# Two Flamingo layers on one core: in layer 1, sums of exponentials added on DVE, block inputs kept in DRAM, a third free PSUM bank

## The chip, the cores and the metric

The kernel runs on one core of a Trainium2 chip. The metric is the device time of one execution in microseconds (us); shorter is better. The time before is the median of three runs, 2996.78 us (2994.19 to 2997.82).

## The reference

The input x holds 8 sequences of 512 tokens with 256 channels in fp32, and a context of 512 tokens with 128 channels for each. Two layers follow each other; each adds a gated attention part and a gated feed-forward part. All of the change lies in layer 1, whose two parts compute, cut to what matters:

```python
def _mha(x, y, ..., causal):
    xn = _ln(x, lnx_g, lnx_b)
    yn = _ln(y, lny_g, lny_b)
    q, k, v = (16 heads of 32 from xn, yn, yn)
    a = softmax(q @ k.T * 32 ** -0.5, axis=-1)
    if causal:
        a = a * mask              # keys t > s are kept; after the softmax, so its sum runs over all keys
    o = a @ v                     # heads side by side: 512 channels
    x_out = x + o @ li1_w + li1_b
    h = gelu(_ln(x_out, ln3_g, ln3_b) @ li2_w + li2_b)      # 256 -> 1024
    return x_out + h @ li3_w + li3_b                        # 1024 -> 256

x = _ln(xx, ln1_g, ln1_b)
x = x + _mha(x, x, a1..., causal=True)       # block 0
x = _ln(x, ln2_g, ln2_b)
x = x + _mha(x, ctx, a2..., causal=False)    # block 1

# feed-forward part of layer 1: quantised 256 -> 1024, a convolution over
# three tokens in each channel, silu, quantised 1024 -> 256
```

## The kernel before

Everything is in fp32 but the quantised products, which are exact in bf16. A sequence's 512 tokens are 4 tiles of 128. Layer 0 is computed first (to about 925 us); what layer 1 needs of it lies in DRAM: `hd` (layer 0's hidden activations), `kd` and `vd` (keys and values of the context for block 1), and the three copies of x in `xd`.

Layer 1 works through 16 slots, one per sequence and block, in the order that `slot_of` gives: sequences 0 and 1 in block 0, the same two in block 1, then 2 and 3, and so on. One slot's attention (`steps1`) has 16 steps: 4 groups `g` of 4 heads, and in each of them 4 key tiles `n`. A step has a front and a back. The front is four products of 32 rows, one per head, into two PSUM tiles `ps_s` of two banks each, then two exponentials on ACT (L2070) into `pt`, a tile of 128 keys x 4 heads x 512 queries (8 KB in each partition, three buffers), and in block 0 a select on POOL (L2074) that masks the diagonal piece into `dg`. The back is, per head, a product of `pt` with 32 columns of ones into `sm` (the softmax's sum, repeated over 32 rows) and the products with the values into `ov`. After the fourth key tile the sum is turned on DVE (L2106), inverted (L2107), turned back (L2109) and multiplied onto `ov` (L2111), which gives `oT`.

Beside the attention run streams of other work, each a generator that yields before it needs something:

- `first(b)`: the end of layer 0's feed-forward part for sequence b; it stores x (`store_x`, L1792).
- `pre1(b, half)`: layer 1's entry for half a sequence: load x, layer normalisation, the block's input `res`, then `enter1`: scale and shift of the normalisation, the inner normalisation, the bias of `li1` added into `res` (L1911), and the turned input `zT`; then the values `vt`.
- `pair1(b, blk, g)`: queries and keys `QT`, `KT` of a head group.
- `mlp1(b, blk, half)`: `oT` times `li1` plus `res` into `xo` (L1978), normalisation, `li2`, gelu, `li3`, added to `res`; at the end of block 0 it goes on through `enter1` to block 1.
- `last(b)`: the feed-forward part of layer 1. A loop over eight channel tiles f: product, scaling into a padded tile `hp` (L2164), and three steps of the convolution (L2167 or L2172, then twice L2176).

`weave_all` puts all of it into one order for each engine while the program is built. It asks a planner (`Pace`) that holds an estimate of when each engine is free, when each tile is done and when the next buffer of a ring is free. Of the candidates that could start within 0.3 us on PE it takes the one with the lowest place: `base + share * done / total` for a stream, the slot and step number for the attention. Where an evacuation may go to ACT or DVE, `sooner` picks by the planner's free times. At most two fronts may be ahead of the backs.

[...] four in `st1` (`ps_s`), two in `ac1` (`sm`, `ov1`), two in `m1a`, the ring `m1` from which `bank()` serves every other product. All DMAs of layer 1 are issued from SP's queue, in program order.

Of the kernel before, what the change touches and what calls it, by code (L numbers as in the profile page):

```python
# [8 lines left out]
F32 = mybir.dt.float32  # L9
# [922 lines left out]
class Fast(General):  # L932
# [8 lines left out]
    def setup(self, ctx, ctx0):  # L941
        super().setup(ctx, ctx0)
        nc, tc = self.nc, self.tc
        dram = ctx.enter_context(tc.tile_pool(name="dram", bufs=1, space=bass.MemoryType.DRAM))

        def scratch(name, shape, dtype=F32):
            return [dram.tile(shape, dtype, name=f"{name}{b}") for b in range(B)]


        self.xd = [scratch(f"xd{k}_", [P, NT * C]) for k in range(3)]  # L950
        self.hd = scratch("hd", [P, NF * T])
        self.cd = scratch("cd", [P, T])
        self.kd = scratch("kd", [P, 4 * T])
        self.vd = scratch("vd", [P, NT * 2 * C])
        self.fwd = {
            n: dram.tile([P, 2 * FF], BF16, name=f"q_{n}")
            for n in ("f0_w1", "f0_w2", "f1_w1", "f1_w2")
        }
        keep = self.keep2
        self.ones = keep.tile([P, 32], F32, name="ones")  # L960
        nc.vector.memset(self.ones, 1.0)


        self.ext = keep.tile([P, 2, 3 * B], F32, name="ext")
        self.n_ext = 0
        self.seqs, self.units, self.given = {}, {}, set()
        self.rest = self.coming = None
        self.behind = Behind()
        self.pace = Pace(tc)
        self.pace.open()  # L970
# [687 lines left out]
    def layer1_xattn(self):  # L1658
        nc, tc = self.nc, self.tc
        with (  # L1660
# [6 lines left out]
            tc.tile_pool(name="m1a", bufs=2, space=PSUM) as self.m1,  # L1667
# [4 lines left out]
            self.hps = [[wpool.tile([P, T // 2 + 2], F32, name=f"hp{k}_{i}") for i in range(2)] for k in range(2)]  # L1672
            for t in self.hps[0] + self.hps[1]:
                nc.gpsimd.memset(t, 0.0)
# [4 lines left out]
            self.li1s, self.mlps, self.loads = [0, 0], [0, 0], {}  # L1679
# [10 lines left out]
            for k, (b, blk) in enumerate(order):  # L1690
                for half in range(2):
                    mlps[half].append(Stream(self.mlp1(b, blk, half), 20.5, 0.88 if blk else 0.65, k + 1))
                    if not blk:
                        pres[half].append(Stream(self.pre1(b, half), 7.5, 0.88, k - 1))
                for g in range(4):
                    pairs.append(Stream(self.pair1(b, blk, g), 3.0, 0.2, k + 0.25 * (g - 1)))
# [100 lines left out]
    def first(self, b):  # L1797
# [32 lines left out]
        yield need(x, pe=False)  # L1830
        self.store_x(1, b, x)
        self.given.add((1, b))
# [40 lines left out]
    def pre1(self, b, half):  # L1873

        while (1, b) not in self.given:
            yield WAIT
# [3 lines left out]
        while b > 2 and self.mlps[half] <= self.slot_of(b - 3, 1):  # L1880
            yield WAIT
        res = q["res", half] = work.tile([P, 2, C], F32, tag=f"res{half}", name="res", bufs=3)
        yield from self.ln_timed(x, res, f"p{half}", of_ln=True)
        yield from self.enter1(b, half, "ln1", "a1", x, f"p{half}")
# [16 lines left out]
    def enter1(self, b, half, ln, pre, z, of):  # L1901
# [3 lines left out]
        res = q["res", half]  # L1905
# [5 lines left out]
        nc.gpsimd.tensor_tensor(res, res, self.row1b(f"{pre}_li1_b"), ALU.add)  # L1911
        blk = int(pre == "a2")
# [13 lines left out]
        if self.both(b, ("zT in", blk)):  # L1926
            q["zT", blk] = zT

# [32 lines left out]
    def mlp1(self, b, blk, half):  # L1961
# [3 lines left out]
        pre = ("a1", "a2")[blk]  # L1965
        while ("oT", blk, 3) not in q:
            yield WAIT
        res = q["res", half]
# [72 lines left out]
        yield from self.enter1(b, half, "ln2", "a2", z, f"m{half}")  # L2041
        self.mlps[half] += 1

    def steps1(self, b, blk):
# [37 lines left out]
        def back(g, n):  # L2082
            self.backs += 1
            kt, pt, parts = st.pop((g, n))
            if n == 0:
                st["sm"] = self.ovp.tile([P, T], F32, tag="sm", name="sm")
                st["ov"] = self.ovp.tile([P, T], F32, tag="ov1", name="ov")
            ov, sm = st["ov"], st["sm"]
            for j in (2, 3, 0, 1):
                self.mm(sm[32 * j : 32 * j + 32, :], self.ones, pt[:, j, :], n == 0, n == NT - 1)  # L2090
            for i, (p, cols) in enumerate(parts):
                for j in (2, 3, 0, 1):
# [5 lines left out]
                    )  # L2098
            if n < NT - 1:
                return  # L2100

# [8 lines left out]
            oT = q["oT", blk, g] = work.tile([P, T], F32, tag="oT", name="oT", bufs=6)  # L2110
# [4 lines left out]
        def back_at(g, n):  # L2115

            if n == NT - 1 and min(self.li1s) < (4 * slot + g - 2) // 4:
                return 1e9
            _, pt, parts = st[g, n]
            t = pace.when([Pace.name(pt), Pace.name(q["vt", blk])] + [Pace.name(p) for p, _ in parts])  # L2120
            return t if n else max(t, pace.place("sm"), pace.place("ov1") - 1.1)
# [7 lines left out]
    def last(self, b):  # L2129
# [25 lines left out]
        for half in range(2):  # L2155

            to = slice(1 - half, n + 2 - half)
            cols = slice(half * (n - 1), half * (n - 1) + n + 1)
            h = work.tile([P, NF, n], F32, tag="hF", name="hF")
            for f in range(NF):  # L2160
                hp = self.hps[half][f % 2]
                yield need(ur, xq, *([h] if f else []))
                ps = self.proj(w1, xq, f * P, cols)
                nc.vector.tensor_tensor(hp[:, to], ps, ur[:, cols], ALU.mult)  # L2164
                a = h[:, f, :]
                if self.pace.sooner(0.47, 0.46):
                    nc.scalar.activation(  # L2167
                        a, hp[:, 0:n], AF.Identity,
                        scale=self.col("conv_w", 3 * f), bias=self.col("conv_b", f),
                    )  # L2170
                else:
                    nc.vector.tensor_scalar(  # L2172
                        a, hp[:, 0:n], self.col("conv_w", 3 * f), self.col("conv_b", f), ALU.mult, ALU.add
                    )
                for k in (1, 2):
                    nc.vector.scalar_tensor_tensor(  # L2176
                        a, hp[:, k : k + n], self.col("conv_w", 3 * f + k), a, ALU.mult, ALU.add
                    )
# [163 lines left out]
```

## Time and profile before

| | us |
|---|---|
| median of three runs | 2996.78 |
| the profiled execution, its own time | 3002.77 |
| its span, from the first to the last instruction | 3001.0 |
| PE busy | 2614.2 (87%) |
| ACT busy | 1488.5 (50%) |
| DVE busy | 1426.5 (48%) |
| POOL busy | 524.2 (17%) |
| PE busy on products with ones (2048 records) | 273.8 |

The profile is of one execution and 6.0 us longer than the median. An fp32 product shows as two records, so the 2048 records are 1024 products, in 256 groups of four [...]. Their busy time counts the stretch in which at least one of them runs; the end of a record is modelled and can lie under the next product. The busy shares are means over stages: up to 800 us layer 0's attention, then layer 0's feed-forward part, from 1000 to 2808 us layer 1 with its attention, then a tail without any.

The page's second part shows the span in 40 slices of 75 us (tenths):

```profile
PE   5999999999682998999988999998989998899842
DVE  2334444434474335334355664345663425665455
ACT  2666665656572445444444545444544344545321
PEclk9999999999896999999999999999999999999965
```

### The profile page before, as it was taken

To read this page: it belongs to the slowest core of one execution; us is meant where nothing else is said; L and a number is where in the kernel's file an instruction comes from. 1 tells how busy PE (TensorE), PEld (TensorE's weight loads), DVE (VectorE), ACT (ScalarE), POOL (GpSimd) and SP (SyncE) were. 2 spreads that over 40 slices of the span, in tenths; PEclk is the share of its full clock that TensorE was granted. 3 is DMA by queue.
4 is the path that set the end of the run, shared out by engine and by line. 5 is a ranking of instruction groups with operands and counts; after the bars stand their busy time and mean duration, and the time that the engine had idled before them with its cause. 6 is when DMAs were issued, how large, how long until landed. Compare 5 with 4: busy or idle time off the path is not lost.

```text
span 3001.0 us, 39948 instructions
## 1 busy us (share of the span) xinstructions
PE 2614.2 (87%) x16359; PEld 1226.4 (41%) x16364; DVE 1426.5 (48%) x2899; ACT 1488.5 (50%) x1817; POOL 524.2 (17%) x687
## 2 busy tenths in 40 slices
PE   5999999999682998999988999998989998899842
PEld 2333333333231344444544435454444454444531
DVE  2334444434474335334355664345663425665455
ACT  2666665656572445444444545444544344545321
POOL 2111111111001224112221111231110201201100
PEclk9999999999896999999999999999999999999965
DMA  3011110100275203201200212110110110110110
GB/s 104 8 40 46 46 40 29 39 15 12 91 308 203 71 15 102 74 22 64 77 27 8 74 56 93 64 43 8 64 39 25 43 57 8 57 46 18 43 35 15
DMA packets 67663, 167.20 MB, mean 56 GB/s; under 512 B 6416, under 2 KB 35472, under 8 KB 59664
## 3 DMA queue, kind: packets, MB, share of 16 engines
q1 hardware_dynamic: 65248, 161.89, 15.4%
q8 instruction: 130, 2.13, 0.3%
q0 software_dynamic: 640, 2.10, 0.2%
q10 hardware_dynamic: 1584, 0.58, 0.1%
q14 instruction: 61, 0.50, 0.1%
HBM read 110.02 MB, written 54.53 MB: 55 GB/s over the span
## 4 chain that ended last, share of the span: by engine, by line
PE 72%; DVE 15%; ACT 7%; issue 3%; DMA 2%; POOL 1%; SPq 0%; ACTq 0%; DVEq 0%; POOLq 0%
PE ps L1010 35%; PE ps_s L1010 17%; PE ov L1010 11%; PE sm L1010 7%; DVE hext L1618 2%; PE ps L1013 2%; DVE hF L2176 2%; ACT pt L1369 1%; ACT pt L2070 1%; DVE mv L1841 1%; DVE hm L2184 1%; ACT hF L2167 1%; DVE oT L2111 1%; DVE hp L2164 1%; DVE rb L2109 1%
## 5 line engine op out<-in xcount | busy, mean ns | idle before, releaser
L1010 PE MATMUL ps_s<-QT,KT 32*128 32x512 f32 (+3 forms) x4096 | 607.0, 611 | 79.6 <-ACT QT L1953 25.7
L2070 ACT ACTIVATE pt<-ps_s 128x1024 f32<-128x1024 f32 x512 | 495.7, 1020 | 303.2 <-PE ps_s L1010 300.3
L1369 ACT ACTIVATE pt<-ps_s 128x1024 f32<-128x1024 f32 (+3 forms) x512 | 411.8, 861 | 206.1 <-PE ps_s L1010 200.3
L1010 PEld LDWEIGHTS ps_s<-QT,KT 32*128 32x128 f32 x4096 | 191.3, 186 | 380.1 <-issue 197.4
L1010 PE MATMUL sm<-pt,ones 128*32 128x512 f32 x2048 | 273.8, 606 | 0.2 <-DVE rt L2106 0.2
L1010 PE MATMUL ps<-x3T,li 128*128 128x256 f32 x1024 | 253.5, 392 | 20.8 <-DVE hD L1652 13.8
L1010 PE MATMUL ov<-pt,v 128*32 128x512 f32 (+3 forms) x2048 | 238.9, 537 | 13.2 <-POOL pt L1372 12.9
L1010 PE MATMUL ps<-li,hD 128*128 128x256 f32 x1024 | 239.1, 387 | 5.6 <-ACT hD L2020 4.3
L1010 PEld LDWEIGHTS ps<-x3T,li 128*128 128x128 f32 x1024 | 186.2, 191 | 106.1 <-issue 37.3
L1010 PEld LDWEIGHTS ps<-li,hD 128*128 128x128 f32 x1024 | 190.9, 191 | 68.0 <-issue 26.2
L1010 PE MATMUL ov<-pt,vt 128*32 128x512 f32 (+3 forms) x1792 | 192.8, 501 | 2.6 <-DVE oT L2111 2.6
L2074 POOL TENSOR_SCALAR_AFFINE_SELECT dg<-pt 128x512 f32<-128x512 f32 x128 | 85.8, 671 | 582.9 <-ACT pt L2070 582.9
L1652 DVE TENSOR_SCALAR hD<-ps,cols 128x256 f32<-128x256 f32 x178 | 81.2, 481 | 203.8 <-PE ps L1010 113.5
L1372 POOL TENSOR_SCALAR_AFFINE_SELECT pt<-pt 128x512 f32<-128x512 f32 x128 | 87.1, 680 | 482.6 <-ACT pt L1369 482.6
L2176 DVE SCALAR_TENSOR_TENSOR hF<-hp,cols,hF 128x256 f32<-128x256 f32 x256 | 131.6, 514 | 61.1 <-ACT hF L2167 54.9
L1847 POOL TENSOR_SCALAR mv<-mv 128x2 f32<-128x2 f32 (+1 forms) x104 | 25.6, 246 | 767.7 <-DVE mv L1842 724.3
L2167 ACT ACTIVATE hF<-hp,cols 128x256 f32<-128x256 f32 x82 | 49.2, 600 | 202.0 <-DVE hp L2164 202.0
L1010 PE MATMUL ps<-zT,a_wq 128*128 128x512 f32 x256 | 130.6, 635 | 9.7 <-DVE hD L1652 5.1
L1010 PE MATMUL ps<-li,oT 128*128 128x256 f32 x512 | 128.7, 395 | 7.5 <-DVE oT L2111 5.9
L1010 PE MATMUL ps<-fw,hq 128*128 128x256 bf16 x512 | 71.5, 300 | 67.1 <-DVE hq L1822 54.6
L1650 ACT ACTIVATE hD<-ps,cols 128x256 f32<-128x256 f32 x78 | 36.6, 473 | 176.1 <-PE ps L1010 152.3
L1394 DVE STREAM_TRANSPOSE ot<-ov 128x512 f32<-128x512 f32 x64 | 45.8, 716 | 158.5 <-PE ov L1010 158.5
(252 smaller groups left out, 3404.7 us busy)
## 6 DMA issues: line engine op xcount, KB each, us to landing
hd<-h SPq DMA_DIRECT2D x16, 1024.0 KB, 3.9
hF<-hd SPq DMA_DIRECT2D x16, 1024.0 KB, 6.5
li<-in_w_a_dram SPq DMA_DIRECT2D x16, 1024.0 KB, 5.0
fw<-q_f_w SPq DMA_DIRECT2D x24, 512.0 KB, 5.8
xF<-xd SPq DMA_DIRECT2D x24, 512.0 KB, 5.1
kd<-k SPq DMA_DIRECT2D x8, 1024.0 KB, 3.9
vd<-v SPq DMA_DIRECT2D x8, 1024.0 KB, 4.4
vt<-vd SPq DMA_DIRECT2D x8, 1024.0 KB, 6.2
```

The lines of the kernel that those rows point to most:

```text
L1010: self.nc.tensor.matmul(out, lhsT, rhs, start=start, stop=stop, skip_group_check=True)
L1013: self.nc.tensor.transpose(out, in_, self.ident)
L1369: nc.scalar.activation(pt[:, 2 * jp : 2 * jp + 2, lo:], pss[jp][:, :, lo:], AF.Exp)
L1372: nc.gpsimd.affine_select(out=diag, in_=diag, compare_op=ALU.is_ge, fill=0.0, base=0, pattern=[[0, 4], [1, P]], channel_multiplier=-1,)
L1394: nc.vector.transpose(ot.rearrange("p b d -> p (b d)"), ov)
L1618: nc.vector.tensor_reduce(e, hh, AX.X, op)
L1650: self.nc.scalar.activation(out, ps, AF.Identity, bias=bias)
L1652: self.nc.vector.tensor_scalar(out, ps, bias, None, ALU.add)
L2070: nc.scalar.activation(pt[:, 2 * jp : 2 * jp + 2, :], pss[jp], AF.Exp)
L2074: nc.gpsimd.affine_select(out=dg, in_=pt[:, :, diag], compare_op=ALU.is_gt, fill=0.0, base=0, pattern=[[0, 4], [-1, P]], channel_multiplier=1,
L2167: nc.scalar.activation(a, hp[:, 0:n], AF.Identity, scale=self.col("conv_w", 3 * f), bias=self.col("conv_b", f),)
L2176: nc.vector.scalar_tensor_tensor(a, hp[:, k : k + n], self.col("conv_w", 3 * f + k), a, ALU.mult, ALU.add)
```

## The change

The sum over key tiles is split: DVE adds the first three `pt` of a head group into a tile of its own, `acc`, and PE multiplies only `acc` and the fourth `pt` with ones, both after the last product with the values. `sm` is no longer a bank of its own; it comes from the ring `m1`, which has three banks now. A `pt` that waits for its add stays in its buffer.

Room in SBUF for `acc` (8 KB in each partition) comes from `res`, which had three buffers for each half: `pre1` and `mlp1` now write the block's input to DRAM (`rd`), and the next `mlp1` loads it into a single buffer; from `oT` (five buffers, not six, with the condition in `back_at` moved by one head group); and from `hp` (two tiles, not four; both halves use the same ones, with the reads shifted by `half` in place of the write). `first` stores each half of x as soon as it is done, and `pre1` waits for its own half. Two shares of the streams change: `mlp1` in block 0 from 0.65 to 0.5, `pre1` from 0.88 to 0.65.

```diff
--- before.py
+++ after.py
@@ -948,6 +948,8 @@
         self.xd = [scratch(f"xd{k}_", [P, NT * C]) for k in range(3)]
+
+        self.rd = scratch("rd", [P, NT * C])
         self.hd = scratch("hd", [P, NF * T])
         self.cd = scratch("cd", [P, T])
         self.kd = scratch("kd", [P, 4 * T])
@@ -1664,19 +1666,19 @@
             tc.tile_pool(name="small2", bufs=1) as self.small,
             tc.tile_pool(name="st1", bufs=2, space=PSUM) as self.st,
             tc.tile_pool(name="ac1", bufs=1, space=PSUM) as self.ovp,
-            tc.tile_pool(name="m1a", bufs=2, space=PSUM) as self.m1,
+            tc.tile_pool(name="m1a", bufs=3, space=PSUM) as self.m1,
         ):
             self.work = work
             self.seqs = {b: {} for b in range(B)}
-            self.hps = [[wpool.tile([P, T // 2 + 2], F32, name=f"hp{k}_{i}") for i in range(2)] for k in range(2)]
-            for t in self.hps[0] + self.hps[1]:
+            self.hps = [wpool.tile([P, T // 2 + 3], F32, name=f"hp{i}") for i in range(2)]
+            for t in self.hps:
                 nc.gpsimd.memset(t, 0.0)
             self.wl = {}
             self.pairs = self.fronts = self.backs = self.zTs = self.nvt = 0
-            self.li1s, self.mlps, self.loads = [0, 0], [0, 0], {}
+            self.li1s, self.mlps, self.loads, self.both_in = [0, 0], [0, 0], {}, {}
             order = [(2 * p + k, blk) for p in range(B // 2) for blk in range(2) for k in range(2)]
             few, pairs, mlps, pres = [], [], [[], []], [[], []]
@@ -1689,9 +1691,9 @@
             few.sort(key=lambda s: s.base)
             for k, (b, blk) in enumerate(order):
                 for half in range(2):
-                    mlps[half].append(Stream(self.mlp1(b, blk, half), 20.5, 0.88 if blk else 0.65, k + 1))
+                    mlps[half].append(Stream(self.mlp1(b, blk, half), 20.5, 0.88 if blk else 0.5, k + 1))
                     if not blk:
-                        pres[half].append(Stream(self.pre1(b, half), 7.5, 0.88, k - 1))
+                        pres[half].append(Stream(self.pre1(b, half), 7.5, 0.65, k - 1))
                 for g in range(4):
                     pairs.append(Stream(self.pair1(b, blk, g), 3.0, 0.2, k + 0.25 * (g - 1)))
             self.weave_all([self.steps1(b, blk) for b, blk in order], [few, pairs, *mlps, *pres])
@@ -1827,9 +1829,8 @@
                     self.mm(ps[:, k, :], hq[:, f, k * P : (k + 1) * P], w2[:, f, :], f == 0, f == NF - 1)
             x2 = x[:, 2 * half : 2 * half + 2, :]
             nc.vector.scalar_tensor_tensor(x2, ps, self.sg, x2, ALU.mult, ALU.add)
-        yield need(x, pe=False)
-        self.store_x(1, b, x)
-        self.given.add((1, b))
+            self.store_x(1, b, x2, half)
+            self.given.add((1, b, half))
     def ln_timed(self, x, out, of, of_ln=False):
@@ -1872,16 +1873,14 @@
     def pre1(self, b, half):
-        while (1, b) not in self.given:
+        while (1, b, half) not in self.given:
             yield WAIT
         nc, work, q = self.nc, self.work, self.seqs[b]
         x = self.load_x(1, b, f"xP{half}", half)
         yield need(x, pe=False)
-        while b > 2 and self.mlps[half] <= self.slot_of(b - 3, 1):
-            yield WAIT
-        res = q["res", half] = work.tile([P, 2, C], F32, tag=f"res{half}", name="res", bufs=3)
+        res = work.tile([P, 2, C], F32, tag=f"resP{half}", name="resP")
         yield from self.ln_timed(x, res, f"p{half}", of_ln=True)
-        yield from self.enter1(b, half, "ln1", "a1", x, f"p{half}")
+        yield from self.enter1(b, half, "ln1", "a1", res, x, f"p{half}")
         while "vt" not in q and (self.nvt < self.slot_of(b, 0) or self.backs < 16 * (self.slot_of(b, 0) - 1)):
             yield WAIT
         if "vt" not in q:
@@ -1898,17 +1897,17 @@
         if self.both(b, "pre1"):
             q["vt", 0] = vt
-    def enter1(self, b, half, ln, pre, z, of):
+    def enter1(self, b, half, ln, pre, res, z, of):
         nc, work, q = self.nc, self.work, self.seqs[b]
-        res = q["res", half]
         nc.vector.tensor_tensor(res, res, self.row1b(f"{ln}_g"), ALU.mult)
         yield need(res, pe=False)
         nc.gpsimd.tensor_tensor(res, res, self.row1b(f"{ln}_b"), ALU.add)
         yield need(res, pe=False)
         yield from self.ln_timed(res, z, of)
         nc.gpsimd.tensor_tensor(res, res, self.row1b(f"{pre}_li1_b"), ALU.add)
+        nc.sync.dma_start(self.half_of(self.rd[b], half), res.rearrange("p t c -> p (t c)"))
         blk = int(pre == "a2")
         while ("zT of", blk) not in q and (self.zTs < self.slot_of(b, blk) or self.pairs < 4 * (self.slot_of(b, blk) - 1)):
             yield WAIT
@@ -1925,6 +1924,7 @@
             nc.vector.tensor_copy(at, ps)
         if self.both(b, ("zT in", blk)):
             q["zT", blk] = zT
+            self.both_in[b, blk] = 2
     def slot_of(self, b, blk):
@@ -1963,9 +1963,12 @@
         nc, work, q = self.nc, self.work, self.seqs[b]
         pre = ("a1", "a2")[blk]
+        while self.both_in.get((b, blk), 0) < 2:
+            yield WAIT
+        res = work.tile([P, 2, C], F32, tag=f"res{half}", name="res")
+        nc.sync.dma_start(res.rearrange("p t c -> p (t c)"), self.half_of(self.rd[b], half))
         while ("oT", blk, 3) not in q:
             yield WAIT
-        res = q["res", half]
         li1 = yield from self.weight("li1", b, blk)
         oT = [q["oT", blk, g] for g in range(4)]
         xo = work.tile([P, 2, C], F32, tag=f"xo{half}", name="xo")
@@ -2038,7 +2041,7 @@
             self.mlps[half] += 1
             return
         yield from self.ln_timed(res, res, f"m{half}")
-        yield from self.enter1(b, half, "ln2", "a2", z, f"m{half}")
+        yield from self.enter1(b, half, "ln2", "a2", res, z, f"m{half}")
         self.mlps[half] += 1
     def steps1(self, b, blk):
@@ -2083,11 +2086,8 @@
             self.backs += 1
             kt, pt, parts = st.pop((g, n))
             if n == 0:
-                st["sm"] = self.ovp.tile([P, T], F32, tag="sm", name="sm")
                 st["ov"] = self.ovp.tile([P, T], F32, tag="ov1", name="ov")
-            ov, sm = st["ov"], st["sm"]
-            for j in (2, 3, 0, 1):
-                self.mm(sm[32 * j : 32 * j + 32, :], self.ones, pt[:, j, :], n == 0, n == NT - 1)
+            ov = st["ov"]
             for i, (p, cols) in enumerate(parts):
                 for j in (2, 3, 0, 1):
                     h = 4 * g + j
@@ -2096,8 +2096,19 @@
                         p[:, j, : cols.stop - cols.start],
                         n == 0 and i == 0, n == NT - 1 and i == len(parts) - 1,
                     )
+
+            if n == 1:
+                st["acc"] = work.tile([P, 4, T], F32, tag="acc", name="acc")
+                nc.vector.tensor_tensor(st["acc"], st["pt"], pt, ALU.add)
+            elif n == 2:
+                nc.vector.tensor_tensor(st["acc"], st["acc"], pt, ALU.add)
+            st["pt"] = pt
             if n < NT - 1:
                 return
+            sm = self.bank()
+            for k, t in enumerate((st["acc"], pt)):
+                for j in (2, 3, 0, 1):
+                    self.mm(sm[32 * j : 32 * j + 32, :], self.ones, t[:, j, :], k == 0, k == 1)
             if g == 0:
                 st["recs"] = work.tile([P, 4, 16], F32, tag="recs", name="recs", bufs=2)
@@ -2107,18 +2118,20 @@
             nc.vector.reciprocal(rec, rt[:, :, 0])
             rb = work.tile([P, T], F32, tag="rt", name="rb", bufs=1)
             nc.vector.transpose(rb, rec.unsqueeze(2).to_broadcast([P, 16, 32]))
-            oT = q["oT", blk, g] = work.tile([P, T], F32, tag="oT", name="oT", bufs=6)
+            oT = q["oT", blk, g] = work.tile([P, T], F32, tag="oT", name="oT", bufs=5)
             nc.vector.tensor_tensor(oT, ov, rb, ALU.mult)
             if g == 3:
                 self.seen(st["recs"])
         def back_at(g, n):
-            if n == NT - 1 and min(self.li1s) < (4 * slot + g - 2) // 4:
+            if n == NT - 1 and min(self.li1s) < (4 * slot + g - 1) // 4:
                 return 1e9
             _, pt, parts = st[g, n]
             t = pace.when([Pace.name(pt), Pace.name(q["vt", blk])] + [Pace.name(p) for p, _ in parts])
-            return t if n else max(t, pace.place("sm"), pace.place("ov1") - 1.1)
+            if n == 0:
+                return max(t, pace.place("ov1"))
+            return max(t, pace.when([Pace.name(st["acc"])]), pace.place("m1")) if n == NT - 1 else t
         return [
             (lambda g=g: front_at(g), lambda g=g, n=n: back_at(g, n),
@@ -2154,27 +2167,26 @@
         n = T // 2
         for half in range(2):
-            to = slice(1 - half, n + 2 - half)
             cols = slice(half * (n - 1), half * (n - 1) + n + 1)
             h = work.tile([P, NF, n], F32, tag="hF", name="hF")
             for f in range(NF):
-                hp = self.hps[half][f % 2]
+                hp = self.hps[f % 2]
                 yield need(ur, xq, *([h] if f else []))
                 ps = self.proj(w1, xq, f * P, cols)
-                nc.vector.tensor_tensor(hp[:, to], ps, ur[:, cols], ALU.mult)
+                nc.vector.tensor_tensor(hp[:, 1 : n + 2], ps, ur[:, cols], ALU.mult)
                 a = h[:, f, :]
                 if self.pace.sooner(0.47, 0.46):
                     nc.scalar.activation(
-                        a, hp[:, 0:n], AF.Identity,
+                        a, hp[:, half : half + n], AF.Identity,
                         scale=self.col("conv_w", 3 * f), bias=self.col("conv_b", f),
                     )
                 else:
                     nc.vector.tensor_scalar(
-                        a, hp[:, 0:n], self.col("conv_w", 3 * f), self.col("conv_b", f), ALU.mult, ALU.add
+                        a, hp[:, half : half + n], self.col("conv_w", 3 * f), self.col("conv_b", f), ALU.mult, ALU.add
                     )
                 for k in (1, 2):
                     nc.vector.scalar_tensor_tensor(
-                        a, hp[:, k : k + n], self.col("conv_w", 3 * f + k), a, ALU.mult, ALU.add
+                        a, hp[:, half + k : half + k + n], self.col("conv_w", 3 * f + k), a, ALU.mult, ALU.add
                     )
             yield need(h, pe=False)
             nc.scalar.activation(h, h, AF.Silu)
```

## The prediction

> **What bounds the kernel now.** I read the page's busy shares first, then the stretches of the span, then the chain of waits inside the long one, and last who waits for whom there. The columns of the windows are busy time with instruction counts in brackets, then granted clock, DMA share and GB/s.
>
> ```profile
> core 0: us, PE busy (x) PEld busy (x) DVE busy (x) ACT busy (x) POOL busy (x), PEclk, DMA share, GB/s
> 1000.00:2808.00 1808.00, 1688.63 (x10790) 849.13 (x10788) 874.84 (x1839) 867.25 (x986) 346.36 (x446) 0.98 0.15 48
> 2808.00:3001.00 193.00, 81.04 (x354) 56.44 (x352) 111.66 (x224) 47.17 (x66) 9.86 (x13) 0.67 0.08 26
> ...
> 1200.00:1600.00 400.00, 386.89 (x2453) 195.71 (x2446) 165.46 (x356) 189.90 (x210) 76.11 (x101) 1.00 0.15 50
> 1600.00:1800.00 200.00, 181.42 (x1133) 85.44 (x1131) 129.80 (x269) 100.10 (x119) 32.81 (x44) 0.97 0.15 49
> ```
>
> Layer 1's attention steps run from 1000 to 2808 us. PE is busy 1688.6 of these 1808 us (idle 119.4), DVE 874.8 (48%), ACT 48%, POOL 19%. TensorE sets this stretch. Inside it there are two kinds: 1200 to 1600 has PE at 97% and DVE at 41%; 1600 to 1800, where the last feed-forward part runs too, has PE at 91% and DVE at 65%. The tail from 2808 on is a chain of DVE, ACT and short PE pieces without attention.
>
> The chain of waits in a piece of the long stretch (start, us, what):
>
> ```profile
> 1337.43 1.91 PE ps L1010 x4
> 1339.35 1.00 PE sm L1010 x8
> 1340.34 0.86 PE ov L1010 x8
> 1341.20 1.92 PE ps L1010 x4
> ```
>
> It is PE on PE without a gap. A group of four products with ones (eight records) is a link of it. Its timeline rows start at 1339.28 (sm) and 1340.16 (ov): 0.88 us. The chain's 1.00 holds some 0.12 us more of changing over, which falls to ov when sm is gone. So 0.88 us is what a removed group gives back, not the 1.07 us that the row calls its duration (its end lies under ov). The page's busy time for sm would say more still: 273.8/2 = 136.9 us for half of it.
>
> Why PE stood still in 1000 to 2808, largest first:
>
> ```profile
> PE ps_s L1010 <- ACT QT L1953: 25.7, 14, 3.3
> PE ps L1010 <- DVE hD L1652: 15.1, 15, 1.7
> PE ps_s L1010 <- ACT KT L1650: 14.0, 6, 3.9
> PE ps_s L1010 <- DVE KT L1652: 13.2, 13, 1.3
> PE ps_s L1010 <- ACT pt L2070: 11.4, 12, 5.2
> PE ps L1010 <- DVE hp L2164: 8.1, 9, 1.1
> ```
>
> With xo (3.6 + 1.6) and res (3.0), the waits for a bank that DVE still empties make 15.1 + 8.1 + 5.2 + 3.0 = 31.4 us.
>
> Two DVE rows price the new work, a two-input operation over 128x2048 (ns min/median/max), and the last links of a head group (us):
>
> ```profile
> L2199 DVE TENSOR_TENSOR hF<-hF,sr x16: 2291/2293/3347, 1590.8 to 2987.1; 128x2048 f32<-128x2048 f32 x16
> ```
>
> ```profile
> 2807.50 0.72 DVE L2106 STREAM_TRANSPOSE rt<-sm 128x512 f32<-128x512 f32 x1 [5.59 <-PE sm L1010]
> ...
> 2809.35 0.69 DVE L2111 TENSOR_TENSOR oT<-ov,rb 128x512 f32<-128x512 f32 x1
> ```
>
> From the end of sm to a free ov bank is 2810.04 - 2807.50 = 2.54 us when nothing lies before it on DVE.
>
> [...] the two-input L2176 is 485 ns in the median and 1473 at most, the select into dg on POOL 637 and 1621. [...]
>
> **The change part by part.**
>
> Ones. A head group has four key tiles, thus four groups of products with ones; now two (the sum of three tiles, and the fourth tile). Layer 1 has 64 head groups: 64 x 2 = 128 groups go, 128 x 0.88 = -112.6 us on PE.
>
> Adds. Two per head group, 128 x 2.291 = 293 us on DVE, which goes from 875 to about 1168 us in a stretch of some 1725: 68%. On average still below PE. In the static order of the two programs the planner moves 34 hD evacuations from DVE to ACT (34 x 0.481 = -16 us), and 23 convolution starts and 14 normalisations the other way (23 x 0.508 + 14 x 0.41 = +17): nothing in sum. 13 more table loads on ACT at 1.283 us = 17 us, ACT being half idle: 0.
>
> What PE feels of the adds. Some 560 DVE instructions of layer 1 empty a bank (hD 144, hp 128, xo and res 64 each, the rest KT, vt, x3T, zT, xF). One of them finds an add running with a chance of 293/1725 = 0.17 and then waits 1.15 us in the mean: 560 x 0.17 x 1.15 = 110 us of late evacuations. No row shows how much reaches PE; bounds 0 (the planner knows each add's length and puts other work first) and +110. A third bank lets PE run one more group ahead, 1.9 us, which covers most of a 1.15 us delay: I take a quarter, +27.
>
> Third bank. It can give back at most the 31.4 us of bank waits, at least 0 (the new sm takes one of the three for two groups and a transpose, 64 times): I take -16.
>
> The ov bank. Before, sm of the next head group ran 0.88 us ahead of its ov and the sum came before the last ov. Now both groups of ones stand after the last ov, and the next ov needs the 2.54 us chain. I laid the trace's durations (ps_s 1.07, a 128x512 pair 1.9, ones 0.88) along the new PE order: in 20 of 63 handovers only 1.1 to 1.7 us of other PE work lie between, short by 23 us together; in 32 it is 3.0 us, just enough. Before, PE waited 2.6 us for oT there. So +20; up to +53 if DVE is 0.6 us late in the tight ones too.
>
> Exponentials. A key tile's buffer (three of them) is now held until its add has run; the fourth tile's exponential waits for the first add. Between them lie ps_s (1.07) and ov (0.97) against 2.29 us. ACT waits some 0.3 us 64 times, a step ahead of its use: +4, bounds 0 and +40. POOL's lock: a select into dg can be 2.3 us late but is used a step later: +3, bounds 0 and +15.
>
> Block inputs through DRAM, with POOL's and SP's part. 32 stores and 32 loads of 256 KB; rows of that size landed in 2.0 us (xd from res) and 5.2 us (xP from xd). On SP the store stands behind POOL's last add into res and the load behind the store and behind the buffer's previous reader; KT, vt and weight loads queue behind them for up to 5 us each. The load is issued before the slot's last head group, steps before xo needs it: 0, bounds 0 and +20.
>
> Start of layer 1. Storing each half lets the first half enter early, but its store now stands on SP ahead of the second half's load of h, which leaves when DVE's L1829 is done (940.57) instead of at 936.08: +4.5 for that half, which then runs with less beside it: 0, bounds -5 and +5. The shares of the streams, one oT buffer less and the two hp buffers: only the order, 0.
>
> Tail. From 2832 to 2853 PE waited 0.86 us before each of eight groups for a bank; with three I take -6 (0 to -9).
>
> Sum: -112.6 + 27 - 16 + 20 + 4 + 3 - 6 = -81 us. Against the profiled execution: span 3001 - 81 = 2920, its own time 3002.8 - 81 = 2922. The median of the runs shown lies 6.0 us lower, so 2996.8 - 81 = 2916.
>
> **The rivals.**
> A, the adds hide: nothing of the 27, 4 and 3, the bank gives 25, the tail 9: -112.6 + 20 - 25 - 9 = -127, 2870. For it: DVE is idle for half of the stretch. Against: idle in DVE's light parts doesn't help its heavy ones.
> B, DVE's load costs as it does in today's heavy parts. Idle PE is 3.3% at 41% DVE and 9.3% at 65%: 0.25 points per point. 20 points more on 1725 us are 86 us in place of 27: -22, 2975. For it: the last part's stretches would have DVE over 80%. Against: much of that idle time is the convolution's own chain, not load.
> C, slower: DVE takes over the path. It works in order, and where the convolution and the adds meet, each add holds hp, hD and the sum's transpose, and with it the PE. From (112.6 + 16 + 6 - 20)/128 = 0.9 us exposed per add it decides. With half of each, 1.15 us: +147 - 115 = +32, 3029. Against: the planner prices the adds.
> That half the ones don't go is excluded: the new order has 512 matmuls with ones in place of 1024.
>
> **How the numbers follow.** Forecast 0.60 (own range 2885 to 2945), A 0.14, B 0.18, C 0.08. The range 2866 to 2972 takes in the forecast, most of A and B, and leaves C out. A measurement of this kernel tells about 0.2%, 6 us, from no change; faster 0.90, same 0.02, slower 0.08.
>
> **What would show it.** Right: sm rows 2048 to 1024 and PE's busy time in the long stretch down by more than 100 us; adds near 2.3 us; PE waits for oT up from 2.6 to 20 or more; waits for hD and hp not above 31. Wrong: adds well over 2.3 us behind POOL, PE idle in the long stretch over 150 us, or SP's queue making xo wait for res.

## The result, and the profile after

The changed kernel takes 2959.1 us (median of four runs, 2957.5 to 2964.2) against 2995.8 beside it: ratio 0.988 (0.9863 to 0.9897). A second comparison, on another chip, gave 0.9855 (0.9826 to 0.9884). That is 37 to 39 us faster, less than half of the 81 forecast; the time lies outside the forecast's own range (2885 to 2945), though inside the wide one (2866 to 2972). The profiled execution took 2964.2 us, its span is 2962.5.

The stretches of the changed kernel, columns as before (the long stretch is now 1000 to 2776):

```profile
core 0: us, PE busy (x) PEld busy (x) DVE busy (x) ACT busy (x) POOL busy (x), PEclk, DMA share, GB/s
1000.00:2776.00 1776.00, 1613.37 (x9758) 841.93 (x9756) 1177.45 (x1972) 874.17 (x995) 443.28 (x447) 0.96 0.17 58
2776.00:2962.00 186.00, 78.94 (x354) 58.08 (x352) 108.88 (x216) 44.17 (x63) 8.76 (x11) 0.67 0.08 26
```

PE's busy time fell by 75 us (1688.6 to 1613.4) where 128 removed groups are 113. Its idle time rose from 119 to 163 us. DVE gained 303 us (293 forecast for the additions); POOL gained 97 us without any new work; the mean granted clock fell from 0.98 to 0.96. The tail is 7 us shorter.

Why PE stood still in that stretch of the changed kernel (in total, times, longest):

```profile
PE ps_s L1012 <- DVE KT L1654: 25.3, 12, 2.9
PE ov L1012 <- DVE oT L2122: 24.8, 19, 2.0
PE ps_s L1012 <- ACT pt L2073: 17.8, 31, 1.7
PE ps L1015 <- ACT z L1854: 17.7, 23, 2.5
PE ps L1015 <- DVE hm L2196: 16.2, 8, 3.4
PE ov L1012 <- POOL dg L2077: 14.7, 11, 2.9
```

DVE's evacuations of hD, 15.1 us of waits before, are gone from the list, as is QT, which led it; hp is down from 8.1 to 2.0 us. The handover of ov (oT) has grown from this line of the kernel before:

```profile
PE ov L1010 <- DVE oT L2111: 2.6, 4, 0.8
```

New, in the last line of the list above, are products that wait for GpSimd's (POOL's) select `dg`. POOL was not on the list before.

The additions, then POOL's two groups in that stretch of the changed kernel, then the same two groups in the kernel before (mean ns after the busy time):

```profile
L2102 DVE TENSOR_TENSOR acc<-pt x64: 2257/2283/2739, 1002.6 to 2767.3; 128x2048 f32<-128x2048 f32 x64
L2104 DVE TENSOR_TENSOR acc<-acc,pt x64: 2257/2281/3983, 1009.0 to 2771.6; 128x2048 f32<-128x2048 f32 x64
```

```profile
L2077 POOL TENSOR_SCALAR_AFFINE_SELECT dg<-pt 128x512 f32<-128x512 f32 x127 | 113.2, 893 | 581.6 <-ACT pt L2073 581.6
L1848 POOL TENSOR_SCALAR mv<-mv 128x2 f32<-128x2 f32 (+1 forms) x83 | 56.3, 679 | 578.8 <-DVE mv L1843 549.2 <-DVE mv L1852 29.4
```

```profile
L2074 POOL TENSOR_SCALAR_AFFINE_SELECT dg<-pt 128x512 f32<-128x512 f32 x128 | 85.8, 671 | 582.9 <-ACT pt L2070 582.9
L1847 POOL TENSOR_SCALAR mv<-mv 128x2 f32<-128x2 f32 (+1 forms) x82 | 19.0, 232 | 545.0 <-DVE mv L1842 530.3 <-DVE mv L1851 14.1
```

In the median an addition takes what the forecast's row said. The select's mean is 893 ns where it was 671, though its median hardly moved (637 ns before, 635 now); a 128x2 operation of a normalisation, 222 ns in the median, has a mean of 679. A few of POOL's operations have become very long. One of them in the timeline of the changed kernel (start, length, engine, and in brackets the wait before):

```profile
1485.07 2.04 PE L1012 MATMUL ps_s<-QT,KT 32*128 32x512 f32 x8 [0.38 <-ACT pt L2073]
1485.96 2.29 DVE L2104 TENSOR_TENSOR acc<-acc,pt 128x2048 f32<-128x2048 f32 x1 [1.12 <-ACT pt L2073]
...
1486.06 3.28 POOL L2077 TENSOR_SCALAR_AFFINE_SELECT dg<-pt 128x512 f32<-128x512 f32 x2 [3.36 <-ACT pt L2073]
...
1488.80 0.66 PE L1012 MATMUL ov<-dg,vt 128*32 128x128 f32 x8 [1.33 <-POOL dg L2077]
...
1490.43 2.09 PE L1012 MATMUL ps_s<-QT,KT 32*128 32x512 f32 x8
...
1492.45 3.38 PE L1012 MATMUL ps<-zT,a_wq 128*128 128x512 f32 x4
```

The add starts at 1485.96, both selects are recorded from 1486.06 and together take 3.28 us instead of 1.27, that is, the first ends only after the add; PE waits 1.33 us for it.

This is no single case. In the changed kernel's trace 17 selects start while an addition runs, and every one of them ends 0.49 us after that addition, whether it started early or late in it. The 16 operations of L1848 that start during an addition all end 0.08 to 0.10 us after it; they took 1.96 to 2.24 us. It works the other way too: where a select started first, in 21 cases, the addition ends 2.14 to 2.25 us after the select. So in this trace the additions and these operations of POOL exclude each other: this is what the prediction calls POOL's lock, and what "the lock" means below.

In the case above PE is slow after its wait: the same group of ps_s took 1.14 us at 1482.76 and takes 2.09 here. The windows around it:

```profile
1485.00:1488.80 3.80, 2.40 (x16) 0.76 (x16) 2.29 (x1) 2.87 (x4) 2.74 (x2) 0.96 0.02 4
1488.80:1495.70 6.90, 6.90 (x24) 2.61 (x24) 0.69 (x1) 1.94 (x2) 1.17 (x2) 0.53 0.00 1
1495.70:1499.60 3.90, 3.86 (x37) 1.37 (x36) 1.56 (x3) 1.23 (x2) 0.00 (x0) 1.00 0.00 0
```

For 6.9 us PE is busy without a gap, at clock 0.53. By the trace's clock records such stretches at half clock add up to 58 us of the long stretch in the kernel before and to 137 us in the changed one. The group of ps_s above took about twice as long at half clock (2.09 against 1.14 us). If all work there did, half of the 79 us added, some 39 us, is extra busy time. That is about what is missing where PE's busy time fell by 75 and not by 113.

### The profile page after: what moved, and what is told of

It reads as the page before. It is cut to its first block, busy times and chain, and to the rows that moved or that the text cites. A ratio compares the mean times of both kernels' runs of the same rounds, so it can differ in the third digit from the quotient of the medians.

```text
span 2962.5 us, 38290 instructions
## 1 busy us (share of the span) xinstructions
PE 2546.4 (86%) x15340; PEld 1224.0 (41%) x15340; DVE 1727.3 (58%) x3028; ACT 1494.9 (50%) x1825; POOL 620.6 (21%) x685
## 5 line engine op out<-in xcount | busy, mean ns | idle before, releaser
L1012 PE MATMUL ps_s<-QT,KT 32*128 32x512 f32 (+3 forms) x4096 | 635.0, 615 | 61.9 <-DVE KT L1654 26.3
L1012 PEld LDWEIGHTS ps_s<-QT,KT 32*128 32x128 f32 x4096 | 199.1, 186 | 415.7 <-issue 236.6
L2077 POOL TENSOR_SCALAR_AFFINE_SELECT dg<-pt 128x512 f32<-128x512 f32 x128 | 113.9, 891 | 595.0 <-ACT pt L2073 595.0
L1012 PE MATMUL ov<-pt,vt 128*32 128x512 f32 (+3 forms) x1792 | 200.5, 519 | 34.8 <-DVE oT L2122 24.8
L1012 PEld LDWEIGHTS ps<-x3T,li 128*128 128x128 f32 x1024 | 196.3, 197 | 56.9 <-issue 16.9
L1848 POOL TENSOR_SCALAR mv<-mv 128x2 f32<-128x2 f32 (+1 forms) x104 | 62.5, 601 | 729.7 <-DVE mv L1843 669.5
L2104 DVE TENSOR_TENSOR acc<-acc,pt 128x2048 f32<-128x2048 f32 x64 | 148.6, 2322 | 6.9 <-ACT pt L2073 6.4
L2102 DVE TENSOR_TENSOR acc<-pt 128x2048 f32<-128x2048 f32 x64 | 150.7, 2355 | 1.0 <-ACT pt L2073 1.0
L1654 DVE TENSOR_SCALAR hD<-ps,cols 128x256 f32<-128x256 f32 x144 | 66.5, 481 | 98.8 <-PE ps L1012 71.8
L1652 ACT ACTIVATE hD<-ps,cols 128x256 f32<-128x256 f32 x112 | 51.2, 472 | 142.0 <-PE ps L1012 74.7
```

The lines of the kernel that those rows point to most:

```text
L1012: self.nc.tensor.matmul(out, lhsT, rhs, start=start, stop=stop, skip_group_check=True)
L1652: self.nc.scalar.activation(out, ps, AF.Identity, bias=bias)
L1654: self.nc.vector.tensor_scalar(out, ps, bias, None, ALU.add)
L1848: nc.gpsimd.tensor_scalar(rstd, mv[:, :, 1], EPS, None, ALU.add)
L2077: nc.gpsimd.affine_select(out=dg, in_=pt[:, :, diag], compare_op=ALU.is_gt, fill=0.0, base=0, pattern=[[0, 4], [-1, P]], channel_multiplier=1,
L2102: nc.vector.tensor_tensor(st["acc"], st["pt"], pt, ALU.add)
```

## The experiments

The kernels with short additions and with a maximum in place of an addition leave out part of the softmax's sum; they are there to measure time alone. All ratios are to the kernel before on the same chip (four chips, with medians of 2998.6 to 3002.4 us for it), with a 95% interval.

**1. Short additions.** Additions of 128x32 in place of 128x2048; the planner is told the full length, so that PE, ACT and POOL have exactly the changed kernel's order. The first of the two additions (the second is cut likewise):

```
-nc.vector.tensor_tensor(st["acc"], st["pt"], pt, ALU.add)
+nc.vector.tensor_tensor(a[:, 0, 0:32], st["pt"][:, 0, 0:32], pt[:, 0, 0:32], ALU.add)
```

> Both additions of a head group act on 128x32 elements in place of 128x2048 (the rest of acc keeps ones, so the sums of the softmax are left out in part); the planner is told the full length, so every engine keeps the order of the changed kernel. Theory W (the adds' time on DVE and their hold on POOL make PE wait, and PE's granted clock falls after such waits): 2890 to 2920 us, PE idle in layer 1's long stretch from 163 to about 110 us, its time at half clock from 137 to 60-90 us. Rival O (the new order itself, ones after the last ov and the single ov bank, costs the missing time): 2945 to 2960 us, half clock above 115 us.

Measured: 2886.9 us, ratio 0.9614 (0.9592 to 0.9635), -115.5 us. So the additions' length costs 76 us (115.5 less the 39.3 of the changed kernel in the later comparison), where the forecast had 27 + 4 + 3 = 34. The time lies a little under the first theory's range. PE in the long stretch, and its waits for KT and dg:

```profile
1000.00:2698.00 1698.00, 1576.83 (x9714) 828.28 (x9706) 906.19 (x1968) 873.18 (x994) 359.47 (x444) 0.97 0.18 61
```

```profile
PE ps_s L1014 <- DVE KT L1656: 14.3, 12, 2.9
...
PE ov L1014 <- POOL dg L2081: 1.8, 1, 1.8
```

**2. The time of DVE without the lock.** In place of each addition stands a maximum over 2048 elements of one `pt`: 2276 ns in the mean, but one operand. The order of PE, ACT and POOL is again that of the changed kernel. The first of the two:

```
-nc.vector.tensor_tensor(st["acc"], st["pt"], pt, ALU.add)
+nc.vector.tensor_reduce(a[:, :, 0], st["pt"], AX.X, ALU.max)
```

> The two additions of each head group are replaced, at the same places of VectorE's queue, by a maximum over the same 128x2048 exponentials, which takes about the same 2.3 us of VectorE but reads one operand; TensorE's order is that of the changed kernel, and the sums of the first three key tiles are left out. Theory D (the additions cost by holding VectorE's queue, and the clock falls after the waits that follow): ratio to the kernel before 0.983 to 0.992, as the changed kernel's 0.988, half-clock time near 137 us. Rival L (they cost by slowing GpSimd, whose selects and residual work then come late): 0.960 to 0.972, as with the short additions (0.961), and GpSimd's selects back near 671 ns.

Measured: 2921.0 us, 0.974 (0.9717 to 0.9763), -77.6 us. It lies between the two ranges expected, so neither theory holds alone: 38 us of the 76 come from DVE's queue being held (from 1 to 2), and 38 from what a two-operand addition does beyond that (from 2 to the changed kernel). Each of these differences carries an uncertainty of some 10 us, by the intervals. PE's stretch, and POOL in this run:

```profile
1000.00:2726.00 1726.00, 1583.61 (x9694) 830.30 (x9688) 1151.24 (x1967) 870.87 (x989) 359.17 (x443) 0.97 0.18 60
```

```profile
L2081 POOL TENSOR_SCALAR_AFFINE_SELECT dg<-pt 128x512 f32<-128x512 f32 x125 | 83.0, 664 | 588.5 <-ACT pt L2077 588.5
L1852 POOL TENSOR_SCALAR mv<-mv 128x2 f32<-128x2 f32 (+1 forms) x83 | 23.6, 284 | 600.2 <-DVE mv L1847 563.6 <-DVE mv L1856 36.5
```

```profile
PE ov L1014 <- DVE oT L2127: 24.0, 19, 2.0
PE ps_s L1014 <- DVE KT L1656: 21.3, 12, 2.9
...
PE ps_s L1014 <- ACT pt L2077: 14.5, 29, 1.2
...
PE ov L1014 <- POOL dg L2081: 1.8, 1, 1.8
```

The select is back at 664 ns and the operation of the normalisation at 284. Here 16 selects start while a maximum runs, and all of them take 0.63 or 0.64 us: the maximum held none of these up. PE's wait for dg is 1.8 us instead of 14.7; those for oT and KT mostly stay.

The maximum differs from the addition in one more way. It reads one `pt` where the addition reads two, so the second tile's buffer comes free earlier: ACT's exponentials wait 44 us for the additions in the changed kernel and 4 for the maxima. Little of this reaches PE, whose waits for pt are 17.8 against 14.5 us. So most of the second 38 us is the lock, and a few us of it may be these buffers.

Since PE's order is the same in these three kernels, their matmuls can be laid side by side, the k-th to the k-th. I took them in groups of 16, from the changed kernel's first product after 1000 us on, and called a group slow where its busy time is over 1.35 times the shortest of the three. All figures are us of the long stretch, except the counts of groups:

```
                    PE idle   at half clock   slow groups   extra time in them   other extra busy time
short additions      121.2        88.7             7               8.8                  10.1
maximum              142.4        99.0             8              10.4                  17.5
changed kernel       162.6       136.5            24              32.2                  17.0
```

Where the groups begin moves the extra times by some 5 us; the picture stays. The queue (first row to second) costs 21 us of waits and few slow groups; the lock (second to third) 20 us of waits, and 15 to 22 us more in slow groups. The time at half clock, which needs no grouping, says the same of the lock: 37.5 us more, half of which is 19.

**3. Shorter locks.** The same additions in two halves, and in four quarters:

```
-nc.vector.tensor_tensor(st["acc"], st["pt"], pt, ALU.add)
+for u in (slice(2, 4), slice(0, 2)):
+    nc.vector.tensor_tensor(st["acc"][:, u, :], st["pt"][:, u, :], pt[:, u, :], ALU.add)
```

> Each addition as two of 128x1024 at the same place (1.2 us each; 20 us more on VectorE in all). Theory L (about half of the additions' cost is that GpSimd is locked out for 2.3 us at a time; now 1.2 us): waits of TensorE for dg from 14.7 to under 9 us, ratio 0.981 to 0.985. Rival D (VectorE's time alone counts): 0.988 to 0.993.

> Each addition as four of 128x512 at the same place (some 0.7 us each; 60 us more of VectorE than whole ones). Theory L: the lock's cost falls on from halves (0.980), VectorE's added time takes some 8 us: 0.977 to 0.982, waits for dg under 4 us. Rival F: no further gain from shorter locks, only VectorE's added time: 0.984 to 0.990.

Measured: halves 2942.6 us, 0.9796 (0.9764 to 0.9827), although the additions keep DVE busy 20 us longer (319 us against 299); quarters 2946.4, 0.9812 (0.9785 to 0.984), no further gain that can be told, with another 21 us of DVE. Waits for dg in the halves run:

```profile
PE ov L1012 <- POOL dg L2077: 2.7, 4, 1.8
```

Halves shift the planner's order a little, so I ran the maximum in halves too, in exactly the halves' order of PE, ACT and POOL:

> The halves run with each half addition replaced by a maximum over the same 128x1024 (one operand, so nothing locks GpSimd out); order of TensorE, GpSimd and ScalarE as in the halves run; the first three tiles' sums are left out. Theory L (the halves gained because the lock is shorter): 0.970 to 0.976, as with the whole maximum (0.974), so that the lock costs half of its former 0.014. Rival F (they gained because VectorE's queue is cut finer, or by the new order): 0.960 to 0.967, the gap of 0.014 to the additions staying.

Measured: 2920.9 us, 0.9719 (0.9692 to 0.9745); whole and halved maxima take the same time (2921.0). So cutting DVE's queue finer gains nothing by itself. The gap between addition and maximum is 41 us for whole ones (2961.8 against 2921.0) and 22 us for halves (2942.6 against 2920.9), each across two chips whose kernels before agree within 2.5 us. So the cost of the second operand falls to about half with half the length of each lock. Quarters don't carry this on: they stay 25 us above the halved maxima on the same chip (2946.4 against 2920.9), with more DVE time and without a maximum in quarters to compare; that part is open. The waits of ACT for the additions are no smaller with halves (52 us against 44), so the buffers are not what the halves gained by.

**4. Telling the planner of the lock.** `self.free["Pool"] = max(self.free.get("Pool", 0.0), end)` after each addition.

> The changed kernel with the planner told that GpSimd is not free before the end of an addition; nothing else. Theory L (late selects are what the planner did not know of): waits for dg from 14.7 to under 7 us and ratio 0.976 to 0.984. Rival R (a new order only moves the waits): 0.985 to 0.995.

> Halves, and the planner told that GpSimd is not free before the end of an addition. Theory L: most of what the planner's knowledge gains (0.004) is already gained by the halves: 0.976 to 0.982. Rival R (order scatter decides): outside of that.

Measured: 2954.9 us, 0.9842 (0.9813 to 0.9871), with waits for dg still at 13.8 us, so what it gains, if anything, doesn't come from where it was expected, and it is not clearly apart from the changed kernel (0.9826 to 0.9884 on one chip). With halves: 2939.5 us, 0.9783 (0.9749 to 0.9816), the fastest run that computes the whole, not to be told apart from halves alone.

> The changed kernel itself, beside the others on the same chip: ratio 0.986 to 0.990.

This was the second comparison of the changed kernel above.

**5. One addition for each head group**, three groups of ones.

```
-            elif n == 2:
-                nc.vector.tensor_tensor(st["acc"], st["acc"], pt, ALU.add)
...
-            for k, t in enumerate((st["acc"], pt)):
+            for k, t in enumerate((st["acc"], st["p2"], pt)):
```

> One addition for each head group in place of two (the first two exponentials), three groups of ones in place of two. Against the changed kernel TensorE gets 64 groups of 0.88 us back, +56 us. Theory D with a cost in proportion to VectorE's added time (79 us for 128 additions): +56 - 40 = +16 us, ratio 0.992 to 0.996. The forecast's price of the additions (34 us): +56 - 17 = +39, ratio 1.001. Rival T (one addition a group is hidden, only the second one in a row is felt): +56 - 79 = -23, ratio 0.979 to 0.983.

Measured: 2972.5 us, 0.9898 (0.9873 to 0.9922), between D and T, nearer D. With short additions this would be some -115.5 + 56 = -59 us; it is -26 (2972.5 - 2998.6). By this estimate the first addition of a group costs 33 us and the second 43. The planner's order is another one here, and orders alone scatter by as much as 1%, so the split is rough; what it speaks against is a free first addition.

**6. The third bank, the order of the ones, a second accumulator.**

`name="m1a", bufs=3` to `bufs=2`:

> The changed kernel with two banks in the ring m1 in place of three (one bank stays unused). Theory W: the waits for hD, hp, xo and res come back (about 30 us) and draw the clock down with them: 2990 to 3010 us. Rival O: the ring hardly matters beside the handover of ov: 2960 to 2975 us.

Measured: 2977.9 us, 0.9906 (0.9886 to 0.9926): the third bank is worth 8 to 15 us, about the forecast's 16 and less than I expected here. Waits for oT rise to 37.8 us. That the sum's bank now competes with everything else would explain it; no run shows that.

Both groups of ones ahead of the last ov, so that the sum's chain starts earlier:

> The two groups of ones stand ahead of the last key tile's ov in place of after it, so the DVE chain to oT begins 0.9 us (block 1) earlier. Theory W: the waits for oT (24.8 us) fall under 12 us and part of the half clock goes: 2930 to 2948 us. Rival O, if the handover were the whole of the missing time: 2905 to 2925 us. If the handover doesn't matter: 2957 to 2965 us.

Measured: 2984.2 us, 0.9937 (0.9916 to 0.9958). A miss: PE's waits for oT grew to 46.7 us, and PE now waits for the second addition (5.5 us for acc). That the ones stand ahead of the last ov, which oT needs as well, fits this, but no run separates it.

The third bank given to a second ov (`bufs=2` on `ov1`):

> The bank taken from the sums goes to a second accumulator of the products with V, and the small ring stays at two banks. To be compared with the changed kernel with a ring of two (0.9906). Theory of the forecast (the single accumulator's handover costs about 20 us, seen as waits for oT of 25 us): waits for oT gone to under 5 us, ratio 0.982 to 0.985. Rival (another wait takes its place, since the same VectorE queue is late anyway): 0.988 to 0.992.

Measured: 3025.7 us, 1.0078 (1.0056 to 1.01). The waits for oT are gone (1.1 us), yet it is 1.7% slower than the comparable 0.9906: PE is busy 1647 us in the stretch against 1616 and idle 182 against 168, with 147 us at half clock against 120. The planner, no longer held back by ov, makes another order; why that one is worse I did not settle.

**7. The housekeeping** (block inputs through DRAM, half stores, shared hp tiles, two shares of the planner), ones and banks as before; then the same with the old shares; then the new shares alone on the kernel before; then the old shares in the changed kernel. The edit of the shares:

```
-self.mlp1(b, blk, half), 20.5, 0.88 if blk else 0.65, k + 1
+self.mlp1(b, blk, half), 20.5, 0.88 if blk else 0.5, k + 1
...
-self.pre1(b, half), 7.5, 0.88, k - 1
+self.pre1(b, half), 7.5, 0.65, k - 1
```

> The kernel before in its sums (sm in its own bank, ones in each step, two banks in m1), with all else of the change: block inputs through DRAM, five oT, two hp, halves stored at once, new shares. Theory W: within 8 us of before (2988 to 3004 us). Rival Q (the DRAM round trips in SP's queue cost the missing time): 3015 to 3035 us.

> The housekeeping run (block inputs through DRAM, shared hp tiles, half stores; ones and banks as before), now with the planner's two shares as before. It was 1.0097 with the new shares. Theory S (the shares made its +29 us): 0.998 to 1.002. Rival M (the block inputs or hp tiles made it): 1.006 or more.

> The kernel before with nothing but the planner's two shares changed (0.65 to 0.5, 0.88 to 0.65). Theory S: 1.007 to 1.012. Rival M: 0.997 to 1.003.

> The changed kernel with the planner's two shares as before (0.65 and 0.88). Theory H1 (the +29 us of the housekeeping run came from the shares, which move layer 1's streams): ratio 0.977 to 0.981. Rival H2 (it came from the block inputs through DRAM and the shared hp tiles): 0.986 to 0.990.

Measured: 1.0097 (1.008 to 1.0114), a miss by 29 us; with the old shares 0.9967 (0.9956 to 0.9978); the shares alone 1.008 (1.0054 to 1.0106); the old shares in the changed kernel 0.999 (0.998 to 1.0), far from both ranges expected. So the DRAM way and the rest are worth 10 us, not nothing, and the new shares cost 24 us in the old layout and gain 33 to 40 (0.999 to 0.988 or 0.9855) in the new one. With the old shares the changed kernel is no faster than the kernel before: its whole gain hangs on the shares.

## Why the prediction was wrong

The direction was right and the size was not, by 42 to 44 us. Its terms without the additions (-112.6 - 16 + 20 - 6 = -115) are what the short additions gave (-115.5). The sum was met, though not each part of it. The shares, put at 0 as "only the order", were worth 33 to 40 us of gain in this layout, and the DRAM way and the rest, also 0, some 10 us in the old one. If such gains simply add up, the other terms gave 40 to 50 us less than their -115, so that agreement is in good part luck. So the shares' 0 was a wrong step too, in the helpful direction, and where those 40 to 50 us went is open.

The step that failed is "POOL's lock: ... +3, bounds 0 and +15". It measured about 38 us, of which a few may belong to the exponentials' buffers. The additions as a whole cost 76 us and not 34, and these 42 us are as much as the whole miss. The prediction had the term and the place, the select into dg, but argued that a select which is late is "used a step later". The trace shows 14.7 us of direct waits for it in 11 places, against 1.8 in one with short additions: there the product stands so close behind its select that a delay of up to 2.1 us (2.76 us for the longest select, against 0.64 in the median) is not covered. Telling the planner of the lock left 13.8 us of them, so its not knowing is not the whole reason; what keeps it from placing other work there stays open. What is shown is that selects which start during an addition end 0.49 us after it, while those that start during a maximum take their usual 0.63 or 0.64 us, that the cost goes away with the second operand, and that it falls to about half (from 41 to 22 us) when the additions are halved; that the maximum also writes less, and whether this adds anything, wasn't separated.

The second thing missing is the clock. No term priced a wait at more than its length. Of the 38 us of the lock, about half (15 to 22 us) are slow groups. In the case above recorded waits of 0.38 and 1.33 us within some 4 us went with 6.9 us at half clock. It is one of several: the changed kernel's long stretch has 27 stretches at half clock, each 3.4 or 6.8 us long. In the 3.4 us before each of them PE was idle for 1.0 to 3.2 us in all. The longest single gap there was never over 3.36 us, and at most 2.03 us in 18 of the 27. So half clock came after waits as short as these, though not after all of them: 53 other pieces of 3.4 us with 0.8 to 1.8 us of idle PE kept the full clock after them. What decides between the two is not shown.

By its other steps. "What PE feels of the adds", +27 with bounds 0 and 110: 38, of which 21 are waits; the largest part of them for KT (14.3 us with short additions, 21.3 with the maximum). Right mechanism, a size too small by 11. The "exponentials" term, +4: ACT waited 44 us for the additions, and PE's waits for pt are 4.8 us longer than with short additions (17.8 against 13.0), so the size fits. The ov bank, +20: the waits for oT went from 2.6 to 24.8 us, in 19 places where 20 were forecast, and are 24.5 with short additions, so they belong to the structure, as argued. What they cost in time isn't shown: the one kernel without them was slower. The third bank, -16: 8 to 15. The tail, -6: -6.5 (193 to 186.5). DRAM loads landed in 2.6 us and nothing waited for them, as argued. Of the signs named, PE's busy time (down by 75 us, where "more than 100" was asked) and "PE idle in the long stretch over 150 us" (163) told at once that it had gone wrong; the adds at 2.28 us and the oT waits were right. Of the rivals, B's 2975 was nearer than the forecast, but its cause, DVE's load alone, is only half of it.

## What to carry to other kernels

Before moving work from TensorE to VectorE, look at what GpSimd does in the same stretch and who waits for it: here 128x2 operations on GpSimd that started during a two-operand addition of 2.28 us on VectorE took 1.96 to 2.24 us in place of 0.22, and cutting the additions in two paid (20 us more of VectorE's time in them, and 19 us less of the whole). Price TensorE's waits with the clock in mind: here about half of the 38 us that the lock cost was slower products and not waits. To find where a cost comes from, keep the order of every other engine and change one instruction's length or its operands; runs that let the planner make a new order scattered by 1% and more.

## What the runs showed that I had not expected

Two shares of the planner, which change no instruction's work, were worth +24 us in one layout and -33 to -40 in the other. A bank that removed 36 us of waits (37.8 to 1.1) made the kernel 1.7% slower. And the whole maximum and the halved one, with 128 more instructions, took the same time on their two chips, with medians 0.1 us apart.
